# A post-norm decoder of two layers on one core: the cross-attentions exponentiate behind the transposes, and all attention transposes become row tiles of 64 queries

## The chip, the core and the metric

The kernel runs on one core of a Trainium2 chip. A core has a matrix engine (PE, whose weight loads are a queue of their own, PEld), a vector engine (DVE), an activation engine (ACT), a general engine (POOL) and SP, which here only issues DMAs. Each engine works through its own instructions in the order in which the program gives them, and engines wait for each other through semaphores. Matmuls read SBUF and write PSUM; PSUM has eight banks of 128 x 512 fp32, which DVE and ACT can read and POOL cannot. The metric is device microseconds of one launch; the kernel before has 820.76 us as the median of three runs (817.53, 820.76, 822.42).

## The reference

Eight sequences (B = 8) of 256 positions and 256 features go through two decoder layers, each with self-mixing, cross-attention and a feed-forward block; behind each of these six blocks stands `x = layernorm(x + block(x))`. Layer 0 mixes by a gated recurrence, and its feed-forward quantises `x` with one scale over the whole batch, so that all eight sequences have to be there before it goes on. Layer 1 has self-attention with relative positions (up to 20 apart) and a gated feed-forward of 768. Both cross-attentions have 16 heads of 16 features over 256 keys:

```python
q, k, v = (query @ Wq.T + bq), (key @ Wk.T + bk), (value @ Wv.T + bv)    # split into 16 heads
scores = einsum('bhqd,bhkd->bhqk', q, k) / 4      # layer 0: + bias[b, q, k], -inf where masked
attn = softmax(scores, axis=-1)
out = einsum('bhqk,bhkd->bhqd', attn, v)          # heads side by side again, then @ Wo.T + bo
```

Inputs and outputs are fp32. There are 3 x 8 x 16 = 384 heads to attend, 256 of them in cross-attentions.

## The kernel before

**Order.** The program is a set of Python generators, one for each piece of work (`recurrence`, `item_x0`, `item_s1`, `item_x1`, `gated`, and what they spawn). Each yields operations with an engine, a cost and the time at which its inputs are ready; `Order.run` picks the next operation by start time and urgency, and so writes the order of all engines before the kernel runs. Costs are figures in the code (`on_pe`, `on_dve`, `on_act`, `TURNS`, and `TURN` for changes of PE's array mode). `Slots` are buffers that operations take and drop; a matmul whose bank is not free in the plan is placed later.

**One attention item** is one sequence in one attention: `item_x0` (layer 0 cross), `item_s1` (layer 1 self), `item_x1` (layer 1 cross). `project_q`, `project_k` and `project_v` make q, k and v. Its 16 heads are four quads of four. In `quad`, one burst of matmuls (L914) computes the scores of four heads at a time as row tiles of 32 (16 features and padding), each head in its own PSUM bank, as queries on partitions x keys along the free axis. One DVE instruction for each 128 queries (L942) then adds the bias or mask, writes the negative-scaled scores to `sn` and their row minimum to `nm`. `head` exponentiates on ACT with `nm` as the bias and with the row sum as accumulator (L958, two instructions and two accumulator reads for a head), transposes the 256 x 256 probabilities with four 128 x 128 PE transposes (`transposed`, L503), and copies the bank to SBUF (`copy`, L291 on DVE or L292 on ACT, whichever the plan has free). `values` (L998) multiplies four heads' transposed probabilities by the values as column tiles of 32. An item's value tile holds a head's 16 columns beside 16 zeros, so that two heads accumulate into one block of 32 rows. The sums go another way: `scales` takes reciprocals (L1022), widens them on POOL (L1028), transposes them (four more at L503) and copies them out; `attend_out` multiplies the output by them (L1050), projects it (L520), adds the residual and normalises (`norm`, L539 to L554). Self-attention has besides two trips through DRAM for relative positions (`to_scratch`, `to_bands`, `tails_task`, `distances`), with POOL work at L1327, L1354, L1410 and L1415.

**Array modes.** Scores use the array as four row tiles (mode s), values as four column tiles (mode v), and everything else, transposes included, as a whole (mode d).

**Loads.** `loads` brings the q and k weights in rows padded to 32 columns for each head (L399) into a probability buffer, and `compact` (L477) takes the padding out on POOL.

Of the kernel before, what the change touches and what calls it, by code (L numbers as in the profile page):

```python
# [19 lines left out]
P = 128  # L20
B = 8
S = 256
# [6 lines left out]
HID = 768  # L29
NH = HID // P  # L30
# [51 lines left out]

WINDOW = 0.1
# [3 lines left out]
class Order:  # L87
# [6 lines left out]
    TURN = {"ds": 0.1, "sd": 0.21, "sv": 0.21, "vs": 0.14, "dv": 0.1, "vd": 0.14}  # L94
# [44 lines left out]
    def run(self):  # L139
        while self.tasks:  # L140
# [3 lines left out]
            for task in sorted(self.tasks, key=lambda t: (t[0] >= FILLER, t[0], t[1])):  # L144
# [3 lines left out]
                if needs:  # L148
                    slots = needs[0].slots
                    if id(slots) in kept:  # L150
                        continue
                    if len(slots.idle) < len(needs):
                        if ready <= self.clock + 0.5:
                            kept.add(id(slots))
                        continue
                    slots.idle.sort()
                    ready = max(ready, slots.idle[len(needs) - 1][0])
# [17 lines left out]
            if best is None:  # L175
                ahead = [t[3][3] for t in self.tasks if t[3][0] == "get" and t[3][3] > self.clock + 0.5]
                if not ahead:
                    raise RuntimeError(f"stuck: {[t[3][:2] for t in self.tasks]}")
                self.clock = min(ahead)
                continue  # L180
            for held in task[3][4]:
                held.take(*held.slots.idle.pop(0))
# [40 lines left out]
def kernel(  # L223
# [42 lines left out]
    p_bufs = slots(work, "p", 3, [P, 4, NQ, S])  # L266
    pts_bufs = slots(work, "pts", 8, [P, NQ, S])
    s_bufs = slots(work, "s", 4, [P, NQ, S])
# [3 lines left out]
    y_bufs = slots(work, "y", 2, [P, NQ, D])  # L272
# [45 lines left out]
    v32s = []  # L318
    for i in range(2):
        t = const.tile([P, NQ, H, 32], F32, name=f"v32_{i}")  # L320
        nc.gpsimd.memset(t, 0.0)
        v32s.append(t)
    v_bufs = kept(v32s)
# [43 lines left out]
    def loads():  # L367
# [15 lines left out]
        for a in range(3):  # L383
            pool = w0 if a == 0 else wts
            for i in range(2):
                o = 2 * a + i
                if o == 2:
                    for b in range(4, B):
# [4 lines left out]
                packed = yield from get(p_bufs, f"wpad{o}")  # L393
                t = packed.tile.rearrange("p k c s -> p (k c s)")[:, 0 : KC * H * 32]
                t = t.rearrange("p (c o) -> p c o", c=KC)
                w = pool.tile([P, KC, D], F32, tag=f"wqk{o}", name=f"wqk{o}")
                ready = yield from dma(
                    [packed.at], 524288,
                    lambda: nc.sync.dma_start(  # L399
                        out=t, in_=chunked(qk_w[o])  # L400
                    ),
                )
                order.spawn(50 + o, compact(o, packed, t, w, ready))
# [70 lines left out]
    def compact(o, packed, t, w, ready):  # L474
        events["wqk", o] = yield from do(
            "POOL", 0.65, [ready],
            lambda: nc.gpsimd.tensor_copy(  # L477
                w.rearrange("p c (h d) -> p c h d", d=DH),
                t.rearrange("p c (h w) -> p c h w", w=32)[:, :, :, 0:DH],
            ),  # L480
        )
        wqk[o] = w
        packed.drop(events["wqk", o])

# [21 lines left out]

    def mm(ps, w, lo, hi, rhs):
# [18 lines left out]
    TURNS = on_pe(4 * 128)  # L526

# [236 lines left out]
    def head_of(n, j):  # L764
        return 8 * (n // 2) + 2 * j + n % 2

    class Item:


        def __init__(self, ai, b, x, source, result):  # L770
            self.ai, self.b, self.x, self.name = ai, b, x, f"{ai}_{b}"
            self.source, self.result = source, result
            self.whole = ai != 1
            self.used = 0
            self.turned = [[] for _ in range(NS)]
            self.t_sums = []

        def key(self, what, *more):
            return (what, self.ai, self.b, *more)

# [86 lines left out]
    def project_v(it, srcT, t_src):  # L867
# [4 lines left out]
        it.v = yield from get(v_bufs, f"v{it.name}", max(t_src, t_w))  # L872
# [6 lines left out]
        def emit(t):  # L879
            flat = v[:, t].rearrange("p h w -> p (h w)")  # L880
            own = bass.AP(
                tensor=flat.tensor, offset=flat.offset,
                ap=[list(flat.ap[0]), [64, H // 2], [48, 2], [1, DH]],
            )
            nc.vector.tensor_tensor(
                own,
                ps.tile[:, t, :].rearrange("p (m i d) -> p m i d", i=2, d=DH),
                rows[2 * ai].rearrange("p (m i d) -> p m i d", i=2, d=DH),
# [8 lines left out]
    def quad(it, n, parts, bias):  # L897


        c, i = divmod(n, 2)  # L900
# [3 lines left out]
        if n == 0 and it.ai != 1:  # L904
            it.sums = small.tile([P, NQ, H], F32, tag="sums", name=f"sums{it.name}")
# [25 lines left out]
        p = yield from get(p_bufs, f"p{it.name}_{n}", t_s)  # L931
        left = [4]
        times = []
        for j in range(4):
            s = yield from get(s_bufs, f"sn{it.name}_{n}_{j}", t_s)
# [4 lines left out]
            def emit():  # L940
                for t in range(NQ):
                    nc.vector.tensor_tensor_reduce(  # L942
                        out=s.tile[:, t, :], in0=ps[j].tile[:, t, :], in1=tile[:, t, :], scale=-1.0,
# [3 lines left out]
            t = yield from do("DVE", 0.7, [t_s, t_b, t_bias, s.at], emit)  # L947
            ps[j].drop(t)
            order.spawn(urgency(it, n), head(it, n, j, p, s, nm, t, left, times))
# [3 lines left out]
    def head(it, n, j, p, s, nm, t, left, times):  # L953
        h = head_of(n, j)

        def emit():
            for q in range(NQ):
                nc.scalar.activation(  # L958
                    p.tile[:, j, q, :], s.tile[:, q, :], AF.Exp, bias=nm[:, q : q + 1], scale=-1.0,
# [3 lines left out]
        t_e = yield from do("ACT", 1.0, [t, p.at], emit)  # L963
        s.drop(t_e)
# [4 lines left out]
        if it.ai == 1 and len(times) == 4:  # L969
            it.tails(n, p, left, max(times))  # L970
# [894 lines left out]
```

## Time and profile before

| What | us |
|---|---|
| median of three runs (lowest, highest) | 820.76 (817.53, 822.42) |
| span of the profiled execution, first to last instruction | 807.4 |
| PE matmul busy | 774.9 |
| DVE busy | 703.4 |
| ACT busy | 629.7 |
| POOL busy | 210.4 |

The profile gives the profiled execution's span and not its whole device time; the three timed runs are 10.1 to 15.0 us longer than that span, the median 13.3. The mean granted clock of PE was 0.998. In the fenced lines below, a group is given as line, engine, operation, tiles and shape, count, then busy time, mean duration of one, and the idle time ahead of it with what ended it; a timeline line is start and length in us, engine, line, operation, tiles, shape, count; a line of the table of stretches has for each engine its busy time and number of instructions. Matmuls are pipelined, so that the duration of one is far more than the time from one start to the next, which is the rate that counts.

### The profile page before, as it was taken

To read this page: it belongs to the slowest core of one execution; us is meant where nothing else is said; L and a number is where in the kernel's file an instruction comes from. 1 tells how busy PE (TensorE), PEld (TensorE's weight loads), DVE (VectorE), ACT (ScalarE), POOL (GpSimd) and SP (SyncE) were. 2 spreads that over 40 slices of the span, in tenths; PEclk is the share of its full clock that TensorE was granted. 3 is DMA by queue.
4 is the path that set the end of the run, shared out by engine and by line. 5 is a ranking of instruction groups with operands and counts; after the bars stand their busy time and mean duration, and the time that the engine had idled before them with its cause. 6 is when DMAs were issued, how large, how long until landed. Compare 5 with 4: busy or idle time off the path is not lost. (4 is left out here: it accounts for less than half of the span.)

```text
span 807.4 us, 21273 instructions
## 1 busy us (share of the span) xinstructions
PE 774.9 (96%) x7175; PEld 597.3 (74%) x7175; DVE 703.4 (87%) x2461; ACT 629.7 (78%) x2036; POOL 210.4 (26%) x398
## 2 busy tenths in 40 slices
PE   7999999999999999997999999999999999999995
PEld 6787777777766787665767677767776767899885
DVE  3998989989787698887799999898898999989986
ACT  2339999899988457786597799999999899845942
POOL 4440321122111044233333304313242323110010
PEclk9999999999999999999999999999999999999999
DMA  5736352100100449889978706743656333100001
GB/s 183 221 120 97 26 74 50 40 15 28 40 14 15 144 116 220 173 166 154 192 159 170 137 7 145 166 87 89 121 120 139 85 72 114 40 15 16 26 14 39
DMA packets 177681, 77.67 MB, mean 96 GB/s; under 512 B 155046, under 2 KB 171430, under 8 KB 177574
## 3 DMA queue, kind: packets, MB, share of 16 engines
q1 hardware_dynamic: 177574, 76.32, 43.4%
q8 instruction: 57, 0.93, 0.5%
q14 instruction: 50, 0.41, 0.2%
HBM read 41.66 MB, written 34.64 MB: 94 GB/s over the span
## 5 line engine op out<-in xcount | busy, mean ns | idle before, releaser
L958 ACT ACTIVATE p<-sn,nm 128x256 f32<-128x256 f32 x768 | 381.5, 510 | 14.1 <-DVE nm L942 8.2
L503 PE MATMUL pt<-ident,p 128*128 128x128 f32 x1536 | 208.4, 278 | 4.3 <-ACT p L958 1.8
L503 PEld LDWEIGHTS pt<-ident,p 128*128 128x128 f32 x1536 | 169.4, 141 | 50.5 <-ACT p L958 30.2
L292 ACT COPY pts<-pt 128x512 f32<-128x512 f32 x277 | 148.3, 591 | 34.5 <-PE pt L503 29.6
L958 ACT ACTIVATION_READ_ACCUMULATOR p<-sn,nm 128x1 f32 x768 | 154.4, 201 | 0.0
L914 PE MATMUL s<-k,q 32*128 32x256 f32 (+2 forms) x1792 | 118.6, 370 | 0.5 <-ACT pts L292 0.3
L998 PE MATMUL pv<-pts,v 128*32 128x256 f32 x1536 | 104.0, 385 | 0.0
L942 DVE CUSTOM_DVE_ANT_0 sn<-s,bias 128x256 f32<-128x256 f32 x256 | 93.1, 419 | 10.0 <-ACT p L958 5.8
L942 DVE CUSTOM_DVE_ANT_0 sn<-s,hide 128x256 f32<-128x256 f32 x256 | 92.8, 418 | 8.2 <-PE s L914 5.3
L942 DVE CUSTOM_DVE_ANT_0 sn<-s,band 128x256 f32<-128x256 f32 x256 | 92.3, 418 | 8.6 <-PE s L914 3.5
L914 PEld LDWEIGHTS s<-k,q 32*128 32x128 f32 x1792 | 77.2, 185 | 30.1 <-issue 20.1
L291 DVE COPY pts<-pt 128x512 f32<-128x512 f32 x107 | 71.1, 683 | 6.7 <-PE pt L503 6.3
L998 PEld LDWEIGHTS pv<-pts,v 128*32 128x32 f32 x1536 | 41.7, 109 | 41.5 <-issue 19.1
L942 DVE DVE_READ_ACCUMULATOR2_ANT nm<- 128x1 f32 x768 | 63.0, 82 | 0.0
L1028 POOL COPY rsw<-rsum 128x512 f32<-128x512 f32 x24 | 14.6, 610 | 157.4 <-DVE rsum L1022 139.0
L520 PE MATMUL pso<-wvo,oT 128*128 128x256 f32 x192 | 46.3, 385 | 0.4 <-ACT pts L292 0.4
L520 PEld LDWEIGHTS pso<-wvo,oT 128*128 128x128 f32 x192 | 35.1, 190 | 7.8 <-issue 1.3
L1354 POOL COPY band<-ends 64x256 f32<-64x256 f32 x64 | 21.5, 360 | 70.8 <-DVE nm L942 70.8
L1426 DVE TENSOR_REDUCE acc<-tail 128x8 f32<-128x864 f32 x32 | 33.4, 1045 | 5.3 <-POOL tail L1415 5.3
L1327 POOL COPY w<-w 128x504 f32<-128x504 f32 x32 | 19.6, 613 | 68.8 <-DVE w L291 40.7
L1709 ACT ACTIVATE sg<-fg 128x512 f32<-128x512 f32 x24 | 14.3, 599 | 21.7 <-PE fg L1698 21.6
L520 PE MATMUL psv<-wvo,ctxT 128*128 128x256 f32 x128 | 30.8, 384 | 0.0
(197 smaller groups left out, 1321.3 us busy)
## 6 DMA issues: line engine op xcount, KB each, us to landing
sk<-w SPq DMA_DIRECT2D x32, 416.0 KB
band<-sk SPq DMA_DIRECT2D x64, 104.0 KB
pb<-p SPq DMA_DIRECT2D x64, 104.0 KB
band<-sk SPq DMA_DIRECT2D x64, 84.0 KB
pb<-p SPq DMA_DIRECT2D x64, 84.0 KB
acc<-pb SPq DMA_DIRECT2D x32, 156.0 KB
ctxT<-in_ctxT SPq DMA_DIRECT2D x16, 256.0 KB
wpad<-in_qk_w SPq DMA_DIRECT2D x6, 512.0 KB
```

What stands on the lines that cost most here:

```text
L291: ("DVE", on_dve(n), lambda: nc.vector.tensor_copy(dst, src)),
L292: ("ACT", on_act(n), lambda: nc.scalar.copy(dst, src)),
L503: nc.tensor.transpose(ps[:, c, t * P : (t + 1) * P], src[:, t, c * P : (c + 1) * P], ident)
L520: nc.tensor.matmul(ps[:, t, :], srcT[:, c, t * P : (t + 1) * P], w[:, c, :], start=(c == 0), stop=(c == KC - 1),)
L914: nc.tensor.matmul(ps[j].tile[:, t, first : first + w], it.q.tile[32 * j : 32 * j + 32, c, t * P : (t + 1) * P], k[32 * j : 32 * j + 32, c ...
L942: nc.vector.tensor_tensor_reduce(out=s.tile[:, t, :], in0=ps[j].tile[:, t, :], in1=tile[:, t, :], scale=-1.0, scalar=3e38, op0=ALU.add, op ...
L958: nc.scalar.activation(p.tile[:, j, q, :], s.tile[:, q, :], AF.Exp, bias=nm[:, q : q + 1], scale=-1.0, accum_out=it.sum_of(q, h),)
L998: nc.tensor.matmul(it.pv.tile[32 * j : 32 * j + 32, c, :], it.v.tile[:, k, head_of(n, j), :], pts.tile[:, k, :], start=(k == 0 and i == 0 ...
L1028: lambda: nc.gpsimd.tensor_copy(wide.tile.rearrange("p t (h d) -> p t h d", d=DH), rs.unsqueeze(3).to_broadcast([P, NQ, H, DH]),),
L1327: nc.gpsimd.tensor_copy(w.tile[:, :, NR:], w.tile[:, :, NR - 1 : NR].to_broadcast([P, HH, PBW - NR]))
L1354: nc.gpsimd.tensor_copy(band.tile[0:BLK, :, t, lo:hi], it.ends[c][0:BLK, t, i:HH:2].unsqueeze(2).to_broadcast([BLK, 4, hi - lo]),)
L1426: lambda: nc.vector.tensor_reduce(acc[:, c, :, own, 1], tail.tile, AX.X, ALU.add),
```

## The change

Three things change together.

In the **cross-attentions**, DVE leaves the scores and the minimum as before, POOL then subtracts the minimum from the scores (`head_whole`), PE transposes the differences, and ACT exponentiates while it empties the PSUM bank, so that exponential and copy are one instruction. Row sums come out of `values` itself: the 16 columns beside a head's values now hold ones, and the two head groups of an item go through the bank one after the other. `divided` turns the result back by DVE's 32 x 32 block transposes, divides, and turns it again; `scales` remains for self-attention alone.

In **all attentions**, the transposes of two heads are one burst of sixteen (`transposed_pair`), each of 64 queries x 128 keys, alternating between the upper and the lower 64 rows of the array, each half with a bank of its own. In the plan this is a mode of its own (t). Self-attention keeps exponential before transposes and plain copies behind them.

**Buffers and loads** follow: in layer 0 the scores live in the probability tiles (12 head slots), in layer 1 cross-attention has four slots, one value tile, one `u` and one `y`; self-attention has value tiles of its own. The weight loads skip the padding in the DMA (two loads for a weight, pieces of 64 bytes) and `compact` goes. `hide` is bf16. The planner no longer lets an operation that lacks a buffer hold others for ever (`patient`). Names of engine choices in `copy` and other either-or operations are unchanged, but the plan is made anew.

```diff
+    ps_tiles = [work.tile([P, 4, NQ, S], F32, name=f"p{i}") for i in range(3)]
+    p_bufs = kept(ps_tiles)
+    early_bufs = kept([t[:, j] for t in ps_tiles for j in range(4)])
+    pts_bufs = slots(work, "pts", 4, [P, 2, NQ, S])
+    late_bufs = slots(work, "s", 4, [P, NQ, S])
...
+    for t in v_tiles:
+        nc.gpsimd.memset(t, 1.0)
...
+    layers = [Layer(2, early_bufs), Layer(1, late_bufs)]
...
-                packed = yield from get(p_bufs, f"wpad{o}")
...
-                order.spawn(50 + o, compact(o, packed, t, w, ready))
+                for c in range(KC):
+                    events["wqk", o] = yield from dma(
+                        [0.0], 131072,
+                        lambda: nc.sync.dma_start(
+                            out=w[:, c, :].rearrange("p (h d) -> p h d", d=DH),
+                            in_=qk_w[o][c * P : (c + 1) * P, :].rearrange(
+                                "p (h w) -> p h w", w=32
+                            )[:, :, 0:DH],
+                        ),
+                        60,
+                    )
...
+    def transposed_pair(ps, srcs):
+        for j, src in enumerate(srcs):
+            for c in range(2):
+                for t in range(2):
+                    for g in range(2):
+                        own = slice(g * BLK, (g + 1) * BLK)
+                        nc.tensor.transpose(
+                            ps[g][:, 4 * j + 2 * c + t, :],
+                            src[own, t, c * P : (c + 1) * P],
+                            ident[own, own],
+                            tile_position=(g * BLK, 0),
+                        )
...
+    PAIR = 0.45
...
+    def head_whole(it, n, j, s, nm, t):
+        def emit():
+            for q in range(NQ):
+                nc.gpsimd.tensor_scalar(
+                    s.tile[:, q, :], s.tile[:, q, :], nm[:, q : q + 1], None, ALU.subtract
+                )
+        t = yield from do("POOL", 0.66, [t], emit)
+        done = it.done[n][j // 2]
+        done.append((j, s.tile, s, t))
+        if len(done) == 2:
+            order.spawn(urgency(it, n), pair(it, n, j // 2, done))
+
+    def pair(it, n, m, done):
+        ps = [Held(banks, f"pt{it.name}_{n}_{m}_{g}") for g in range(2)]
+        pts = Held(pts_bufs, f"pts{it.name}_{n}_{m}")
...
+        for g in range(2):
+            dst = halves_of(pts.tile)[g]
+            if it.whole:
+                t = yield from do(
+                    "ACT", on_act(512), [t_p, pts.at],
+                    lambda: nc.scalar.activation(dst, parts(g), AF.Exp, scale=-1.0),
+                )
+            else:
+                t = yield from copy([t_p, pts.at], dst, parts(g))
...
     def values(it, n):
+        if it.whole and n == 2:
+            t_turned = yield from event(it.key("turned", 0))
+            t_v = max(t_v, t_turned)
...
+    def divided(it, i, t):
...
+            lambda: nc.vector.transpose(
+                u[:, :, i : i + 2, :].rearrange("p n a d -> p n (a d)"),
+                it.pv.tile.rearrange("p c (n e) -> p (c n) e", e=32),
+            ),
...
+            nc.vector.reciprocal(it.rec[:, i, :], u[:, :, i + 1, 0])
+            nc.vector.tensor_tensor(
+                u[:, :, i, :], u[:, :, i, :],
+                it.rec[:, i, :].unsqueeze(2).to_broadcast([P, NB, DH]), ALU.mult,
+            )
...
+            lambda: nc.vector.transpose(
+                it.oT.tile.rearrange("p c (n e) -> p (c n) e", e=32),
+                u[:, :, 0:2, :].rearrange("p n a d -> p n (a d)"),
+            ),
...
+        t = t_pv
+        if ai == 1:
+            t = yield from event(it.key("scales"))
```

## The prediction

> **What bounds the kernel now.** I read the busy times first, then the table of stretches (start, layer 0, the barrier of the quantiser, layer 1), then the order of time on PE, then the groups.
>
> ```profile
> PE 774.9 (96%) x7175; PEld 597.3 (74%) x7175; DVE 703.4 (87%) x2461; ACT 629.7 (78%) x2036; POOL 210.4 (26%) x398
> ```
> ```profile
> 56.60:277.00 220.40, 216.59 (x1941) 161.76 (x1941) 188.44 (x742) 194.06 (x646) 38.82 (x55) 1.00 0.23 47
> ...
> 300.00:807.40 507.40, 485.68 (x4874) 373.59 (x4872) 451.43 (x1565) 406.69 (x1333) 139.37 (x283) 1.00 0.51 107
> ```
>
> Columns of the second are PE, PEld, DVE, ACT, POOL. PE stands still for 4 us of layer 0 and 22 us of layer 1. But busy counts the time a matmul is in the pipe, so what PE needs must come from the spacing of starts:
>
> ```profile
> 561.11 0.60 PE L503 MATMUL ps_rs<-ident,rsw 128*128 128x128 f32 x4
> 561.64 1.15 PE L914 MATMUL s<-k,q 32*128 32x256 f32 x16
> 562.71 1.07 PE L998 MATMUL pv<-pts,v 128*32 128x256 f32 x16
> 563.71 2.02 PE L503 MATMUL pt<-ident,p 128*128 128x128 f32 x16
> 565.57 1.27 PE L1317 MATMUL psr<-drel,q 128*128 128x328 f32 x4
> ```
>
> Sixteen transposes take 1.86 us from start to start, four 0.53: 0.11 each, plus about 0.09 on leaving the mode. Sixteen score matmuls (four row tiles at a time) take 1.07, that is four rounds of 0.215 plus 0.21; sixteen value matmuls 1.00, four rounds plus 0.14. Each change of mode thus costs 0.14 to 0.21. Summing all of PE's instructions at such spacings (0.11 a transpose, 0.216 a full fp32 pass of 256 columns, 0.86 a burst, 0.118 in the feed-forward, plus 343 changes of mode), I get 738 of 807: 47 at the start, 205 of layer 0's 220, 29 around the barrier, 457 of layer 1's 507. PE is the bound; 69 us are lost in waits, and DVE at 87% is the next bound.
>
> **The change, part by part.** Counts are from the two programs' instruction lists.
>
> *Transposes, all attentions.* 1,536 of 128 columns go (1,536 x 0.108 = 166 us), 3,072 of 64 columns come, two row tiles at a time. The scores show that row tiles run together, loads included: four row tiles of 256 columns per 0.215 us. Streaming 64 columns takes half of 0.108; so a pair of heads is eight rounds of 0.054 = 0.43. The load might bind instead:
>
> ```profile
> L503 PEld LDWEIGHTS pt<-ident,p 128*128 128x128 f32 x1536 | 169.4, 141 | 50.5 <-ACT p L958 30.2 <-issue 7.0 <-ACT pts L292 4.2
> ...
> L1468 PEld LDWEIGHTS psa<-ident,acc 128*82 128x82 f32 x128 | 13.0, 120 | 7.1 <-issue 4.0 <-DVE nm L942 0.9 <-PE pt L503 0.5
> ```
>
> 46 columns more cost 21 ns, so 128 columns fill about 58 ns; I take 0.06 for a round, 0.48 for a pair, 192 x 0.48 = 92. Saved: 74. Bounds: 83 (stream alone) and nothing (no overlap: 16 x 0.054 = 0.86, as today).
>
> Against this stands the Trainium skill, "TensorE: Matmul & The Clock Gate", LDWEIGHTS: loading time goes by columns at 1.2 GHz and not by rows, so half-height tiles load no faster. By that rule a round would be 107 ns, a pair 0.86, and this term zero. The transposing loads above grow at half that price for a column, which is why I go by them.
>
> *Sums from ones.* 64 transposes of `ps_rs` go: 7 us of PE. POOL's widening (16 x 0.61) and its latency go too. The value matmuls are as many as before.
>
> *Changes of mode.* With bursts t apart from d, the lists have 449 changes instead of 343. 106 x 0.15 to 0.21: +16 to +22, taken as 18. Sum on PE: -74 - 7 + 18 = -63, of which a third in layer 0 and two thirds in layer 1; 738 becomes 675.
>
> *DVE.* Net time of one is taken from busy over count in the groups. Gone: 71 of 107 probability copies (0.62 each, 44 us), 16 multiplications by the sums (10), 16 reciprocals (5), and some 45 copies and biases that the plan moves to ACT (0.4 to 0.7, about 31). Added: 48 block transposes of 128x512, 32 reciprocals of 16 columns, 32 multiplications of 256. No row shows a block transpose; rows of that size run from 0.60 (copies) to 1.0 (`acc<-tail`, a reduction of 864); I take the copy, which moves as many elements. 48 x 0.6 + 32 x (0.15 + 0.35) = 45 (bounds 40 and 65). Net -45: 703 becomes 658.
>
> *ACT.* 512 exponentials with accumulator reads (0.50 each, 257) and about 185 copies (0.5, 90) go; 256 exponentials out of PSUM come at 0.57 (row `sg<-fg`, same size, 599 ns): 146. ACT falls by some 200, to about 430; it no longer ends any wait for long.
>
> *POOL.* 512 subtractions of 128x256 with a scalar for each partition. The nearest rows:
>
> ```profile
> L684 POOL TENSOR_SCALAR a<-z x8: 617/618/1657, 9.1 to 80.8; 128x512 f32<-128x512 f32 x8
> ```
> ```profile
> L1058 POOL TENSOR_TENSOR xb<-x_l1a,rows 128x512 f32<-128x512 f32 x8 | 10.2, 1276 | 0.0
> ```
>
> One input: 0.62 for 512, and 0.19 for two columns at L544, so 0.40 for 256 or 0.34 back to back. Two inputs: 1.28, so 0.73. The scalar isn't a stream, so I take 0.34: +174, POOL about 365. Upper bound 374.
>
> *What POOL does to DVE* is the term I trust least.
>
> ```profile
> 120.30 1.27 POOL L1153 TENSOR_TENSOR bias<-bias,neg 128x512 f32<-128x512 f32 x1
> 120.36 1.68 DVE L554 TENSOR_SCALAR xn<-xb,mv_l0x,rs_l0x 128x256 f32<-128x256 f32 x2 [0.57 <-POOL rs_l0x L549]
> ...
> 121.97 0.72 DVE L554 TENSOR_SCALAR x_l0x<-xb,mv_l0x,rs_l0x 128x256 f32<-128x256 f32 x2
> ```
> ```profile
> L554 DVE TENSOR_SCALAR x_l1a<-xb,mv_l1a,rs_l1a x16: 401/408/1942, 380.0 to 679.7; 128x256 f32<-128x256 f32 x16
> ```
>
> The pair of scalings that began just behind a POOL instruction took 1.68, its twin 0.72: it waited until POOL was done. Once (380 us, the 1,942) it sat through four POOL instructions in a row. L942, which reads PSUM, takes 0.418 whether POOL is busy or not. The Trainium skill, "GPSIMD Engine Reference", Specifications, agrees: the two engines share their SBUF interfaces when DVE uses both ports or has two SBUF inputs. About 16 of some 130 such DVE instructions were held here, 0.7 us each, with POOL 26% busy (18% in layer 0). After, POOL is busy for half to three quarters of these stages, and 32 multiplications with two SBUF inputs join the exposed. I expect three times the cases: about 35 us instead of 11, so +25 on DVE (0 to 90, the latter if each exposed group waits for a quad's subtractions). 658 + 25 = 683 DVE beside 675 PE.
>
> *Waits added.* `head_whole` stands in POOL's queue between `norm`'s roots, `w`, `band` and `tail`; PE's pair waits for two heads instead of one; the third quad's values wait for a DVE block transpose of the first half; the output of an item waits for a second chain on DVE, some 2.0 us instead of 0.6. The plan fills PE with other items meanwhile, except behind the last item: +1.5.
>
> *Loads.* Each q or k weight becomes 4,096 packets of 64 bytes instead of 256 of 2 KB. Packets of 80 bytes took 12 ns on one of 16 DMA engines, so 3.1 us instead of 1.3, and one more issue of 0.5 on SP. Two weights lie ahead of the 24 bias loads, six ahead of the context (issued at 34.3, then about 9 us later). In the new list the whole recurrence stands ahead of the first `psk`, 52 us of PE work, which hides it; uncovered it would cost up to 9. Taken as 0. The feed-forward's `sg` has four slots instead of eight, for three a sequence: nothing.
>
> **The sum.** 807.4 - 63 (PE) = 744. In this span DVE would be 92% busy instead of 87%, and its queue is in order; with the tail I add 5: 749. The three timed runs lie 13.3 (median) above the span, so 762; I say 760.
>
> **Rivals.**
>
> 1. *Row tiles don't pay* (slower). If loads or streams of the two halves take turns, a pair costs 0.86. For it: no row shows a transposing row tile. Against it: the score bursts. Price: -7 + 18 = +11, 832. It decides from 0.81 us a pair on.
> 2. *DVE is held at its port.* With POOL's runs of subtractions unbroken, 60 to 90 us of holding: DVE's 718 to 748 is then the bound; with some 55 us that it can't use (16 of the first 57, the barrier, the end, waits for PE) and the 13.3: 786 to 816.
> 3. *POOL becomes the bound.* At the two-input price a head takes 1.46: in layer 0, 128 x 1.46 + 39 = 226 us, more than before's whole stage of 220, which then saves nothing (about 40 lost against the forecast); layer 1 has 326 of 460. 800 to 812.
> 4. *Better.* The 69 us of waits shrink too, since ACT's 30 us of holding up transposes (the idle time at L503) is relieved: 725 to 742.
>
> **How the numbers follow.** Forecast (742 to 786) 0.52, rival 1 0.12, rival 2 0.17, rival 3 0.09, rival 4 0.10. A measurement of this kernel tells about 0.5% (4 us) from no change. Faster: all but rival 1, less a little where 2 and 3 overrun: 0.84; within 0.5% 0.04; slower 0.12. The range leaves out rival 1 above and half of rival 4 below: 728 to 820.
>
> **What would show it.** Right: bursts of 16 half-height transposes with starts 0.5 us or less plus 0.1 apart; layer 0 from first scores to last about 180 instead of 220; POOL's subtraction at 0.34 to 0.40; ACT near 430. Wrong: a pair at 0.8 or more; a subtraction of 0.6 or more, with PE waiting for POOL at the transposes; many L596 scalings (today L554) above 1 us. I would be most wrong if the shared port holds DVE in every item, or if transposing tiles take turns.

## The result, and the profile after

The changed kernel takes 1011.46 us (median of 4 runs, 1007.98 to 1013.99), the kernel before beside it 820.08 (817.53 to 822.42): a ratio of 1.232, 95% interval 1.227 to 1.237. The forecast was 760, with a range up to 820. It was wrong by the sign.

The page of the changed kernel: busy times, the slices of PE, POOL and PE's clock, and the head of the chain that ended last.

```profile
PE 837.9 (83%) x8647; PEld 591.8 (59%) x8647; DVE 677.8 (67%) x2408; ACT 450.3 (45%) x1142; POOL 664.7 (66%) x887
...
PE   8987687888779888988878889788877877889885
...
POOL 3459999999999614433494585956839668633851
PEclk9998888888878899999989979899999976999988
...
POOL 15%; PE 14%; DVE 6%; issue 3%; ACT 3%; DMA 1%; SPq 0%; POOLq 0%; DVEq 0%; ACTq 0%
```

No engine is above 83% of the span, and yet the time is longer: the work waits. POOL, at 26% before, is at 66%, and full from the fourth to the thirteenth slice, which is layer 0. The chain's largest part is POOL's. The table of stretches (start, layer 0, the barrier, layer 1; columns PE, PEld, DVE, ACT, POOL, granted clock, DMA share, GB/s), cut at the first and last score matmul of layer 0 and at the first of layer 1:

```profile
0.00:67.10 67.10, 59.08 (x276) 47.23 (x276) 47.92 (x113) 18.73 (x41) 24.83 (x44) 1.00 0.64 126
67.10:326.00 258.90, 203.78 (x2173) 137.47 (x2172) 147.37 (x643) 86.95 (x172) 244.71 (x274) 0.85 0.17 33
326.00:392.30 66.30, 55.40 (x367) 41.23 (x359) 44.61 (x124) 24.82 (x41) 28.20 (x43) 0.95 0.29 93
392.30:1009.10 616.80, 519.63 (x5845) 365.90 (x5844) 437.87 (x1530) 319.83 (x888) 366.96 (x528) 0.91 0.45 86
```

Layer 0 and layer 1 of the kernel before, cut in the same way:

```profile
56.60:248.40 191.80, 190.55 (x1772) 142.11 (x1772) 170.53 (x686) 176.04 (x600) 35.42 (x50) 1.00 0.23 42
...
307.60:807.40 499.80, 478.76 (x4841) 368.21 (x4840) 443.86 (x1545) 401.60 (x1320) 134.51 (x269) 1.00 0.51 106
```

From first to last score layer 0 takes 259 us instead of 192 (the prediction's 220 runs on beyond the last score), and POOL is busy for 245 of them. In layer 1 POOL is busy for 367 of 617, so there it is not full, but that stage took 500 us before. The lines of the new step, by groups (out<-in, shapes, count | busy, mean ns of one | idle before, releaser) and by line (minimum, median, maximum), and what PE's loads waited for (us in all, times, longest):

```profile
L1018 POOL TENSOR_SCALAR sn<-sn,nm 128x256 f32<-128x256 f32 x256 | 234.0, 932 | 47.1 <-DVE nm L1000 47.1
...
L1018 POOL TENSOR_SCALAR p<-p,nm x256: 912/921/1102, 68.9 to 342.1; 128x256 f32<-128x256 f32 x128
```
```profile
PEld pt L536 <- POOL p L1018: 48.6, 77, 0.9
PEld pt L536 <- POOL sn L1018: 44.7, 71, 1.4
```

A subtraction takes 0.92 us, not 0.34. A head has two: 1.84. Layer 0's 128 heads make 235 us, with the 39 of POOL's other work 274; the subtractions of layer 0 run from 68.9 to 343. So POOL sets layer 0's pace, and the transposes wait for POOL in both layers. That is the sign that the prediction named for its own failure.

### The profile page after: what moved, and what is told of

It is laid out like the page before. It is cut to its first block, busy times and chain, and to the rows that moved or that the text cites. A ratio compares the mean times of both kernels' runs of the same rounds, so it can differ in the third digit from the quotient of the medians.

```text
span 1009.1 us, 23722 instructions
## 1 busy us (share of the span) xinstructions
PE 837.9 (83%) x8647; PEld 591.8 (59%) x8647; DVE 677.8 (67%) x2408; ACT 450.3 (45%) x1142; POOL 664.7 (66%) x887
## 5 line engine op out<-in xcount | busy, mean ns | idle before, releaser
L1018 POOL TENSOR_SCALAR sn<-sn,nm 128x256 f32<-128x256 f32 x256 | 234.0, 932 | 47.1 <-DVE nm L1000 47.1
L1018 POOL TENSOR_SCALAR p<-p,nm 128x256 f32<-128x256 f32 x256 | 233.4, 930 | 12.9 <-DVE nm L1000 12.9
L1045 ACT ACTIVATE pts<-pt 128x512 f32<-128x512 f32 x256 | 137.1, 597 | 210.8 <-PE pt L536 208.0
L536 PE MATMUL pt<-ident,p 64*128 64x64 f32 x2048 | 109.9, 238 | 48.9 <-POOL p L1018 33.6
L536 PEld LDWEIGHTS pt<-ident,p 64*128 64x128 f32 x2048 | 83.9, 144 | 91.7 <-POOL p L1018 48.6
L1060 ACT ACTIVATE p<-p,nm 128x256 f32<-128x256 f32 x256 | 127.0, 506 | 8.3 <-POOL tail L1554 4.2
L1000 DVE CUSTOM_DVE_ANT_0 p<-s,band 128x256 f32<-128x256 f32 x256 | 92.3, 417 | 11.3 <-PE s L966 6.3
L536 PE MATMUL pt<-ident,sn 64*128 64x64 f32 x1024 | 65.3, 250 | 41.5 <-POOL sn L1018 32.4
L1000 DVE CUSTOM_DVE_ANT_0 p<-s,bias 128x256 f32<-128x256 f32 x256 | 91.8, 416 | 11.7 <-PE s L966 11.5
L318 ACT COPY pts<-pt 128x512 f32<-128x512 f32 x92 | 49.2, 587 | 10.0 <-PE pt L536 9.7
```

What stands on the lines that cost most here:

```text
L318: ("ACT", on_act(n), lambda: nc.scalar.copy(dst, src)),
L536: nc.tensor.transpose(ps[g][:, 4 * j + 2 * c + t, :], src[own, t, c * P : (c + 1) * P], ident[own, own], tile_position=(g * BLK, 0),)
L1000: nc.vector.tensor_tensor_reduce(out=dst[:, t, :], in0=ps[j].tile[:, t, :], in1=tile[:, t, :], scale=-1.0, scalar=3e38, op0=ALU.add, op1=A ...
L1018: nc.gpsimd.tensor_scalar(s.tile[:, q, :], s.tile[:, q, :], nm[:, q : q + 1], None, ALU.subtract)
L1045: lambda: nc.scalar.activation(dst, parts(g), AF.Exp, scale=-1.0),
L1060: nc.scalar.activation(p.tile[:, j, q, :], p.tile[:, j, q, :], AF.Exp, bias=nm[:, q : q + 1], scale=-1.0, accum_out=it.sum_of(q, h),)
```

## The experiments

All times are compared with runs of the kernel before on the same chip (812 to 814 us there, 820 beside the changed kernel, so that across chips the ratios are to be compared). Where a kernel keeps "the changed order", only the instruction that is emitted differs; the planner's list is the same.

| run | what | median us | ratio to before, 95% |
|---|---|---|---|
| changed kernel | | 1011 | 1.227 to 1.237 |
| e1 | no subtraction, changed order | 848 | 1.034 to 1.048 |
| e2 | subtraction of a constant | 967 | 1.184 to 1.195 |
| e3 | subtraction on ACT | 923 | 1.127 to 1.139 |
| e4 | before, with row tiles alone | 830 | 1.016 to 1.025 |
| e5 | e4's order, transposes of 128 rows | 827 | 1.014 to 1.023 |
| e6 | e1, order planned without the step | 813 | 0.998 to 1.003 |
| e7 | e1's order, transposes of 128 rows | 845 | 1.037 to 1.046 |
| e8 | fast form on POOL | 839 | 1.029 to 1.039 |
| e9 | e4 with seven banks | 875 | 1.070 to 1.082 |
| e10 | before with seven banks | 843 | 1.032 to 1.042 |
| e11 | e4's order, DVE relieved | 802 | 0.983 to 0.990 |
| e12 | e8 without row tiles | 824 | 1.013 to 1.017 |
| e13 | e5's order, DVE relieved | 809 | 0.995 to 0.999 |
| e14 | e4's order, ACT relieved | 823 | 1.010 to 1.017 |

### Is it the subtraction alone, and is it the scalar?

My first theory was that the scalar for each partition made the instruction slow and that the rest of the forecast held. Three edits of the changed kernel, each in its order:

```diff
-                nc.gpsimd.tensor_scalar(s.tile[:, q, :], s.tile[:, q, :], nm[:, q : q + 1], None, ALU.subtract)
e1: (nothing in its place)
e2: +            nc.gpsimd.tensor_scalar(s.tile[:, q, :], s.tile[:, q, :], 0.0, None, ALU.subtract)
e3: +            nc.scalar.activation(s.tile[:, q, :], s.tile[:, q, :], AF.Identity, bias=nm[:, q : q + 1], scale=-1.0)
```

> The changed kernel without POOL's 512 subtractions: the exponential is taken of the bare scores, so the subtraction of each query's minimum is left out; plan, order and all other instructions stay. Theory (the subtraction's 0.92 us alone turned the gain into the loss): the rest of the prediction holds, POOL near 200 us, layer 0 near 180 us from 60 to 240, mean granted clock back at 0.98 or more, time 735 to 785 us. Rival A (row tiles, mode changes or the longer chains lose the time, the subtraction only lies beside it): 850 us or more. Rival B (the lower granted clock is a cause by itself, brought by the row tiles): clock near 0.90, time 800 to 900.

> The same 512 subtractions on POOL, same tiles in place, but of the constant 0.0 in place of each partition's own scalar (the minimum is thus not subtracted). Theory (it is the scalar for each partition that costs 0.92 in place of 0.34): 0.32 to 0.42 us each, POOL 365 to 400 us, time 750 to 800, and its distance to the run without any subtraction is what POOL's work does to DVE (forecast 25 us, bounds 0 to 90). Rival C (the price is due to the tile's place, its size, or to sharing SBUF with DVE): 0.8 to 0.95 us each and a time within 3% of the changed kernel's 1011.

> The subtraction on ACT in place of POOL (Identity of -1 times the score plus the minimum, 128x256, the sign of the exponential turned to match), plan and order as in the changed kernel. Theory: 0.40 to 0.50 us each as ACT's exponentials with a bias took in the kernel before, ACT 450 + 205 to 256 = 655 to 705 us, POOL near 200, time 760 to 830: better than before or level with it. Rival A: 870 or more. If ACT's in-order queue holds up the transposes, PE waits for ACT at the half-height loads, and the time lies between, 830 to 870.

e1 came to 848, e2 to 967, e3 to 923. Both halves of the theory fell. The subtraction of a constant is nearly as slow (0.85), and its median lies 12 ns above its minimum, so that waiting for something else isn't what makes it long:

```profile
L1018 POOL TENSOR_SCALAR p<-p x256: 840/852/1038, 69.1 to 325.5; 128x256 f32<-128x256 f32 x128
```

And without any subtraction the kernel is still 4% slower than before, where I had expected 7% faster. So of 23 points of loss 19 are POOL's step, and from there to the forecast are another 11. The granted clock is 0.966 to 0.988 in the four executions of e1, with the same row tiles and changes of mode, against 0.896 to 0.910 in the changed kernel: most of the lost clock comes with the subtraction and not with the row tiles. On ACT the step takes 0.44 each (225 us of busy time over 512) and moves the loss to another queue, where it stands ahead of the exponentials (ACT 645 us).

### What makes the POOL instruction slow?

Behind the last store of the kernel before, 54 POOL instructions on tiles that nothing else uses, and the same again beside DVE:

```diff
+            for i in range(6): ts(256, True, 0.0, None, ALU.subtract, None)
+            for i in range(6): ts(256, True, 1.0, 0.0, ALU.mult, ALU.add)
+            for i in range(6): ts(256, True, ptr, None, ALU.subtract, None)
+            for i in range(6): ts(256, True, ptr, -1.0, ALU.subtract, ALU.mult)
...
```

> The kernel before with 108 POOL instructions behind its last store, on two tiles that nothing else uses by then: six each of nine forms on 128x256 or 128x512 fp32, once with DVE idle and once beside DVE scalings of 128x512 in SBUF (its total time is longer by these and says nothing). Theory 1 (one operation alone is slow on POOL, two are fast): subtract alone 0.84 to 0.92 us and add alone the same, multiply-add and subtract-multiply 0.34 to 0.40, with DVE idle. Theory 2 (the operation subtract is slow): add alone 0.34 to 0.40, subtract and subtract-multiply 0.84 or more. Theory 3 (sharing SBUF with DVE): all 256-element forms 0.34 to 0.45 with DVE idle, subtract 0.84 to 0.92 beside DVE. Theory 4 (256 elements have a fixed price whatever the form): all 256-element forms 0.84 or more, 512-element multiply-add 0.62.

Lines of the loop's one source line, each cut to a stretch: multiply-add with constants, subtraction of a partition's scalar, that and a multiplication, the lone addition (with one instruction of a neighbour form in some stretches, seen in the minimum or maximum). The last two are multiply-add and subtraction beside DVE:

```profile
L1781 POOL TENSOR_SCALAR v<-v x7: 407/408/851, 811.8 to 815.2; 128x256 f32<-128x256 f32 x7
L1781 POOL TENSOR_SCALAR v<-v,cols x6: 924/924/926, 815.7 to 820.8; 128x256 f32<-128x256 f32 x6
L1781 POOL TENSOR_SCALAR v<-v,cols x7: 925/1147/1155, 820.8 to 828.1; 128x256 f32<-128x256 f32 x7
L1781 POOL TENSOR_SCALAR v<-v x7: 622/851/864, 838.4 to 843.8; 128x256 f32<-128x256 f32 x6, 128x512 f32<-128x512 f32 x1
L1781 POOL TENSOR_SCALAR v<-v x7: 453/455/974, 865.4 to 869.2; 128x256 f32<-128x256 f32 x7
L1781 POOL TENSOR_SCALAR v<-v,cols x6: 1040/1045/1045, 869.7 to 875.4; 128x256 f32<-128x256 f32 x6
```

Multiply-add of 256 elements takes 0.41; a lone addition or subtraction, in place or not, 0.85; with a scalar for each partition 0.92; with a multiplication behind the subtraction 1.15; a tensor minus a tensor 0.72. None of my four theories is right as it stood: one operation is slow, but so is the pair of subtract and multiply; of the forms tried only multiply and add is fast. DVE beside it adds 0.05 to 0.12. The row from which the prediction took its price, `a<-z`, was a multiply-add.

So the same result can be had from the fast form: -1 times the value plus the minimum, with the exponential's sign turned. The plan also gets a price of 1.1 a head:

```diff
-                    s.tile[:, q, :], s.tile[:, q, :], nm[:, q : q + 1], None, ALU.subtract
+                    s.tile[:, q, :], s.tile[:, q, :], -1.0, nm[:, q : q + 1], ALU.mult, ALU.add
-        t = yield from do("POOL", 0.66, [t], emit)
+        t = yield from do("POOL", 1.1, [t], emit)
-    nc.scalar.activation(dst, parts(g), AF.Exp, scale=-1.0)
+    nc.scalar.activation(dst, parts(g), AF.Exp, scale=1.0)
```

> The changed kernel in full, with one instruction form changed: POOL computes minimum minus value as a multiplication by -1 and an addition of the partition's scalar, in one instruction, and the exponential's sign is turned. The plan gives this step 1.1 us a head instead of 0.66. Theory (POOL has a fast multiply-add, and a lone operation is slow): 0.42 to 0.52 us each as the constant multiply-add showed 0.41 to 0.46, POOL near 430 us, 815 to 850 us in all. Rival (the scalar for each partition spoils the fast form): 0.9 us or more each, 940 to 1010.

839 us, and the whole computation is there. Its group and its line of busy times:

```profile
L1018 POOL TENSOR_SCALAR sn<-sn,nm 128x256 f32<-128x256 f32 x256 | 124.0, 502 | 45.6 <-DVE nm L1000 45.0
```
```profile
PE 761.4 (91%) x8647; PEld 556.0 (67%) x8647; DVE 680.8 (81%) x2419; ACT 442.1 (53%) x1130; POOL 442.8 (53%) x888
```

This one form (with its price in the plan) takes the ratio from 1.232 to 1.034, some 160 us. An order planned at 1.84 a head for the slow form wasn't tried, so the share of the plan in this stays open.

### Do the row tiles pay?

e4 is the kernel before with one part of the change, the pairs of heads turned in row tiles. e5 and e7 keep the orders of e4 and e1 and only turn the 16 half-height transposes of a pair back into eight of 128 rows (which also changes the banks: one for each head instead of two shared, still taken as a pair):

```diff
-                    for g in range(2):
-                        nc.tensor.transpose(ps[g][:, 4 * j + 2 * c + t, :], src[own, t, c * P : (c + 1) * P],
-                            ident[own, own], tile_position=(g * BLK, 0))
+                    nc.tensor.transpose(ps[j]..., src[:, t, c * P : (c + 1) * P], ident)
```

> The kernel before with one part of the change alone: all attention transposes as row tiles of 64 queries, two heads to a burst, with the changed kernel's planner. Exponential on ACT ahead of them, sums and everything else as before. Its list has 472 changes of mode against 343. Theory (row tiles pay, 0.48 to 0.54 a pair): PE's need 738 - 74 + 22 = 686 us, DVE unchanged near 703 and now the bound, time 765 to 805. Rival (a pair costs 0.81 or more): 835 or more.

> The row-tile-alone kernel's list and order, with its 192 pairs of bursts turned back into transposes of 128 rows (each head into one of the pair's two banks): PE's demand is about 50 to 70 us higher, all other engines' instructions are equal. Theory (PE isn't the one bound; PE, DVE and ACT hold each other up through the eight PSUM banks and their queues, and a saving on PE alone passes through for a fifth to a half): 840 to 865 us against 830. Rival (PE bounds, as the prediction had it, and row tiles pay in full): 885 or more. Rival (row tiles don't pay at all): 825 to 835.

> The changed kernel's list without the subtraction (848 us), its half-height pairs turned back into transposes of 128 rows in the same order. Theory (PE isn't the one bound): 855 to 880. Rival (row tiles pay in full wherever they stand): 905 or more. Rival (they don't pay at all): 843 to 853.

e4 took 830, e5 827; e7 845 against e1's 848. Both pairs came out at the last of the rivals, "don't pay at all". e5, which has whole transposes as the kernel before, is 1.8% slower than it, so pairs and the order planned for them cost about as much as e4 lost. On PE itself the row tiles do what was forecast. The same stretch in time order (start, us from first to last end, operation), e4 first, e5 second:

```profile
527.30 0.71 PE L524 MATMUL pt<-ident,p 64*128 64x64 f32 x16
527.93 0.82 PE L1364 MATMUL psr<-drel,q 128*128 128x328 f32 x2
528.68 0.75 PE L524 MATMUL pt<-ident,p 64*128 64x64 f32 x16
529.37 2.14 PE L945 MATMUL s<-k,q 32*128 32x256 f32 x16
...
532.44 0.27 PE L524 MATMUL pt<-ident,p 64*128 64x64 f32 x1
533.60 0.71 PE L524 MATMUL pt<-ident,p 64*128 64x64 f32 x15 [0.89 <-DVE w L301]
```
```profile
526.58 1.09 PE L522 MATMUL pt<-ident,p 128*128 128x128 f32 x8
527.50 0.72 PE L1358 MATMUL psr<-drel,q 128*128 128x328 f32 x2
528.06 1.04 PE L522 MATMUL pt<-ident,p 128*128 128x128 f32 x8
529.02 1.76 PE L939 MATMUL s<-k,q 32*128 32x256 f32 x16
```

From start to next start a pair takes 0.63 to 0.69 in row tiles and 0.92 to 0.96 in whole transposes, the change of mode included; 192 pairs make some 54 us of PE. In e4 they don't reach the end. The last two lines of e4 show one way: a first half-height transpose runs into one bank of its pair, then PE stands still for 0.89 us until DVE has emptied the other (the copy to `w`). PE's busy time is only 19 us lower (765 and 784), since it counts waits within the pipe and time at a lower clock.

The clock takes a part. All executions of e4 have a mean granted clock of 0.965 to 0.976, those of e5, in the same order, 0.986 to 0.994; some 0.02 of 825 us, 16 us, is an estimate of the most that this can cost. e1 and e7 have one pair of executions at the same clock: 839.8 us at 0.988 with row tiles, 844.7 at 0.986 without. The other three of e1 have 0.966 to 0.978 and 846 to 852 us. So at the same clock the row tiles bring 5 us there, and none in the medians. Why the row-tile runs get less clock isn't shown. Twice, in two different orders, 54 us of PE's work are worth 0 to 5 us, to which the lost clock can add a part but not the whole.

### What binds, if not PE?

From the traces I worked out for each PSUM tile the time from its first matmul to the end of its last reader, and so how many of the eight banks are held (the first two columns from 400 to 700 us of each run, the last over the whole run):

| | mean banks held | time with 7 or 8 held | one `pt` bank held, us |
|---|---|---|---|
| before | 5.5 | 28% | 1.70 |
| e4, row tiles | 6.0 | 45% | 2.15 |
| e5, pairs, whole transposes | 5.7 | 34% | 1.89 |
| e12, single heads, whole transposes | 5.5 | 35% | 1.61 |

A quad of scores takes four banks at once; a row-tile pair takes two at once, where the kernel before took one for each head. To see whether that matters, one bank was taken away from e4 and from the kernel before, each planned anew:

```diff
-    banks = slots(psum, "bank", 8, [P, 2, 256])
+    banks = slots(psum, "bank", 7, [P, 2, 256])
```

> The row-tile-alone kernel, planned with seven PSUM banks instead of eight. Theory (banks hold the row-tile order up: two are taken at once for a pair, four at once for a quad's scores): 845 to 875, a loss of 2 to 5% on 830, and more than the kernel before loses by the same. Rival (banks don't bind): 836 or less.

> The kernel before, planned with seven PSUM banks instead of eight. Theory (banks bind less here, since each head's transposes take one): 820 to 840 against 812. Rival (banks don't bind): 816 or less. If it loses as much as the row-tile kernel or more, pairs are not worse off than single heads.

875 against 830 is +5.4%; 843 against 813.6 is +3.7%. The kernel with pairs loses more, as expected, but the kernel before is bound by banks too, more than I had thought. Both were planned anew, so that a part of either loss, and of the 1.7 points between them, may be the order.

Then the other engines were relieved, with row tiles in place. For DVE the reduction runs over a quarter of the columns (the exponential then takes no minimum off, a line not shown here); for ACT the cross-attentions' sums are not kept:

```diff
e11, e13: -  out=s.tile[:, t, :], in0=ps[j].tile[:, t, :], in1=tile[:, t, :], scale=-1.0,
e11, e13: +  out=s.tile[:, t, 0:64], in0=ps[j].tile[:, t, 0:64], in1=tile[:, t, 0:64], scale=-1.0,
e14:      -  accum_out=it.sum_of(q, h),
e14:      +  **({} if it.ai != 1 else dict(accum_out=it.sum_of(q, h))),
```

> The row-tile-alone kernel in its own order with DVE relieved: the reduction that adds the bias and finds the minimum runs over 64 of 256 columns, the rest keeps old values, and the exponential takes no minimum off (so three quarters of the scores and the minimum are left out). DVE falls by some 130 to 160 us of 713, and a bank of scores comes free sooner. Theory (with PE relieved DVE and the banks that it frees are what binds): 740 to 785. Rival (what binds is the length of the chains or ACT): 805 or more.

> The row-tile-alone order with DVE relieved (three quarters of the scores and the minimum left out, as in the run of 802 us), and its pairs turned back into transposes of 128 rows in the same order. Theory (PE takes over as soon as DVE and the banks are relieved, so row tiles pay then): 815 to 850. Rival (PE's need doesn't count even then): 797 to 808.

> The row-tile-alone kernel in its own order with ACT relieved: the exponentials of the two cross-attentions keep no sums (512 accumulator reads of 0.2 us left out, the sums are ones), so ACT falls by about 103 us of 624 and PE has the row tiles. Theory (chains through eight banks bind, and ACT's time lies in a chain of every head): 805 to 820. Rival A (ACT doesn't count): 826 to 834. Rival B (ACT is the bound): 770 or less.

In e11 DVE fell from 713 to 576 us and ACT from 624 to 558: 802, that is 28 us for 138 of DVE's and 66 of ACT's together. In e13, the same with whole transposes, 809: now the row tiles are worth 8 us. In e14 ACT fell by 42 (624 to 583; the 512 reads are 103 by their own records, but an exponential with one behind it costs only 0.08 more) and the time by 7. All three came out between the numbers of my theories. No single engine binds this kernel: 54 us of PE bring 0 to 5 (8 with DVE relieved), 138 of DVE with 66 of ACT 28, 42 of ACT 7, while one bank in eight costs 45 with the row tiles and 30 without. That more banks would let the row tiles pay can't be tried; there are eight. A version in which a head's transposes need no second bank wasn't tried.

### The order, and the whole change without row tiles

e6 is e1 planned with no cost for the missing step; e12 is e8 with single heads and whole transposes (and POOL's step planned at 1.0 us a head instead of 1.1):

```diff
e6:  -        t = yield from do("POOL", 0.66, [t], emit)
e6:  +        t = yield from do("POOL", 0.0, [t], lambda: None)
e12: -        ps = [Held(banks, ...) for g in range(2)]   # a pair
e12: +        ps = Held(banks, f"pt{it.name}_{n}_{j}")     # a head
e12: +        t_p = yield from do("PE", TURNS, [t, ps], lambda: transposed(ps.tile, src))
```

> The changed kernel without the subtraction of the minimum, as before, but with the planner told that this step costs nothing, so that the order of the work is made for it. Theory (some of the 848 us of the same kernel with the order planned for 0.66 us a head is a wrong order): 815 to 835. Rival (the order isn't what is lacking; the rest of the change just doesn't shorten layer 1): 840 to 855.

> The changed kernel with the fast form on POOL and without row tiles: exponential behind the transposes and sums from ones as in the change, each head turned by four transposes of 128 rows into one bank of its own. Planned anew, with 1.0 us a head for POOL. Theory (row tiles give nothing back and their pairs hold more banks): 805 to 830, below the 839 of the same kernel with row tiles. Rival (PE's saving is what carries this kernel): 855 or more.

e6 takes 813, level with the kernel before (0.998 to 1.003). So 4 points of e1's loss, some 33 us, were an order made for a step that wasn't there. What is left is telling:

```profile
PE 746.0 (92%) x8647; PEld 545.8 (67%) x8647; DVE 671.3 (83%) x2410; ACT 443.6 (55%) x1135; POOL 198.8 (24%) x374
...
67.10:307.50 240.40, 222.34 (x2533) 159.56 (x2532) 197.86 (x775) 106.71 (x206) 40.43 (x60) 0.98 0.25 63
307.50:811.60 504.10, 464.00 (x5845) 338.38 (x5844) 425.54 (x1524) 318.11 (x888) 133.89 (x271) 0.99 0.48 104
```

By busy time PE has 29 us less than in the kernel before, DVE 32, ACT 186, POOL 12, the minimum isn't even subtracted, and the span is 811.6 instead of 807.4. e12 takes 824 against e8's 839: with POOL's step at its fair price, the change is better off without row tiles (the two are planned separately, so a part of the 15 us may be the order). No version that does the whole work beats the kernel before.

## Why the prediction was wrong, step by step

In shares of the time before, the way from the forecast to the result has three parts: forecast 0.926; the same work with its order planned right and POOL's step free 1.001 (e6); planned for 0.66 us a head 1.041 (e1); with POOL's real price 1.232. So 7.5 points are a saving that never came, 4 an order, 19 POOL's instruction.

- **POOL: wrong, and the largest error.** "The scalar isn't a stream, so I take 0.34", with 0.73 as the upper bound. It measured 0.92, and POOL is busy for 665 us in place of 365. The step that failed is the choice of the nearest row: `a<-z` has the same engine, type and kind of instruction, but its operations are multiply and add, the one pair that m1 shows to be fast. The bound from a two-input row was no bound: a lone subtraction is slower than subtracting a tensor (0.72). The Trainium skill, "GPSIMD Engine Reference", Engine selection, holds that elementwise work is about twice as slow there as on VectorE with two inputs, and roughly at line rate with one; the multiply-add agrees with that (0.41, as DVE's scaling of 128x256), the lone operations (0.85, against 0.72 for two inputs) do not, and the measurement decides.
- **Rival 3** had the mechanism: POOL as the bound, layer 0 at heads times price plus 39, PE waiting at the transposes. Its formula with 1.84 in place of 1.46 gives 274, as measured. It stopped at 812 because its price did, and because it took layer 1 as free while POOL isn't full there. It isn't: 617 us in place of 529 (e1), since the step lies in every head's chain and the order was made for 0.66.
- **The sum: wrong.** "807.4 - 63 (PE) = 744". This step failed too. PE was 96% busy with 69 us of waits, and I took its whole saving off the span; with POOL's step free nothing of it came (e6). PE did get shorter; but DVE at 87% with its queue in order, and eight banks, were limits at nearly the same place. The working checked only that DVE would be 92% busy in the new span, and never asked what each PSUM bank is doing, although the change took them two at a time. The Trainium skill says it, in "TensorEngine Tiling (Array Packing)", Gotcha 1: row tiling raises the pressure on PSUM, since different row tiles need different banks. The runs agree: a `pt` bank is held 2.15 us instead of 1.70, and one bank fewer costs 5.4% with pairs and 3.7% without. How much of the missing saving is due to banks, how much to the queues of DVE and ACT and how much to the clock stays open: DVE and ACT, relieved, gave back only a part. The 13.3 us between span and time are no part of a launch either: in every run that has both on record the time is 1.7 to 3.0 us above the span of the same execution, so the span of 807.4 belongs to another execution than the three times. The forecast's ratio hardly moves by it (749 of 807 is 0.928, 760 of 820.76 is 0.926).
- **Transposes: right.** A pair was taken as 0.48. Bursts of 32 half-height transposes take 1.14 from start to next start and bursts of 16 0.64, so 0.50 for one more pair and 0.14 for the change of mode. Rival 1 (a pair at 0.81 or more) is false as a mechanism; that the time comes out as if it were true has another cause.
- **Changes of mode: right**, 449 as counted, at 0.14.
- **DVE: right by luck**, by two errors that cancel. 683 was forecast and 678 measured. The hold at the port, "the term I trust least" at +25, was taken first of all from scalings that begin beside POOL's TENSOR_TENSOR. Beside the subtraction the same scaling is hardly held. Its line and one instance, in the changed kernel and then in e1, which has no subtractions:

```profile
L596 DVE TENSOR_SCALAR y<-xb,mv_l0x,rs_l0x x16: 406/540/582, 126.6 to 364.3; 128x256 f32<-128x256 f32 x16
126.58 1.86 POOL L1018 TENSOR_SCALAR p<-p,nm 128x256 f32<-128x256 f32 x2
126.61 1.04 DVE L596 TENSOR_SCALAR y<-xb,mv_l0x,rs_l0x 128x256 f32<-128x256 f32 x2 [7.86 <-POOL rs_l0x L591]
```
```profile
L596 DVE TENSOR_SCALAR y<-xb,mv_l0x,rs_l0x x16: 401/1353/1359, 102.1 to 279.7; 128x256 f32<-128x256 f32 x16
102.08 1.27 POOL L1287 TENSOR_TENSOR bias<-bias,neg 128x512 f32<-128x512 f32 x1
102.14 2.63 DVE L596 TENSOR_SCALAR y<-xb,mv_l0x,rs_l0x 128x256 f32<-128x256 f32 x2 [0.91 <-POOL rs_l0x L591]
```

  So in the changed kernel 48 scalings of L596 take 0.52 to 0.54 in median in place of 0.41, some 6 us; none takes above 0.8. Against e1 all of DVE's groups that became longer make 9 us. In e1 the scaling to `y` costs 10 us more than in the changed kernel, since it begins beside POOL's TENSOR_TENSOR. What decides whether POOL holds DVE isn't shown. And the net of the change is -24 (e1) instead of -45. That scaling makes 11 of the difference (18.2 us, against 6.8 for `xn` before), the multiplications by the reciprocals 4 (0.47 each, not 0.35), the reciprocals 3 (0.25, not 0.15), and the block transposes 5 (34.1 for 48; the 16 of the second kind take 11.3). The copy that their price was taken from is 0.66 by its row (71.1 over 107), not 0.60 or 0.62:

```profile
L1126 DVE STREAM_TRANSPOSE u<-pv 128x512 f32<-128x512 f32 x32 | 22.8, 712 | 44.0 <-PE pv L1095 44.0
```
- **ACT: nearly right**, 450 for 430 (the exponential out of PSUM takes 0.60, as the row quoted, 599 ns, had it, and not 0.57). Its 180 us bring nothing by themselves, as the prediction's rival 4 would have needed.
- **Waits (+1.5) and loads (0).** The first score comes 10.5 us later, since the whole recurrence stands ahead of it, and the first score of layer 1 in e6 at 307.5 as before (307.6). Ahead of the first score PE stands still for 7.5 us in e6 and for 6.1 before, so that by busy time the loads cost little if anything; that they are hidden altogether isn't shown.

## What to carry to other kernels

Take a price only from a row with the same operations, not just the same engine, size and type; if there is none, no other row bounds it, as 0.73 did not bound 0.92; a step that lies in every item's chain should then be measured first. Before a saving on a 96% busy engine is taken off the span, list what else is nearly as busy (here DVE at 87%) and what is taken in groups (here PSUM banks), and ask which of them the change takes more of. In a kernel whose order is made by a planner, a wrong price is paid twice: in the instruction, and in the order of everything else.

## What the runs showed of the hardware

- POOL's fp32 instruction with scalars depends on the operations: multiply-add on 128x256 0.41 us (0.47 to 0.50 with a scalar for each partition, beside other work), a lone add or subtract 0.85, with a partition's scalar 0.92, subtract and multiply 1.15; on 512 elements 0.62 for multiply-add, 1.56 for the subtraction of a scalar.
- Two transposing row tiles of 64 fp32 rows run side by side, loads included: eight rounds in 0.50 us, 62 ns a round, half of 0.108 a transpose of 128 rows and a little more.
- DVE beside POOL lengthens POOL's instructions by 0.05 (multiply-add) to 0.12 us (subtraction).
- A DVE scaling of 128x256 in SBUF (0.41 us alone) that began beside POOL's TENSOR_TENSOR took 1.35 (e1); beside POOL's subtraction it took 0.54, at most 0.58 (changed kernel).
